# Graph attention and propagation in fp32: one ring of row tiles, a new table layout, and a new order of all steps

## The chip, the cores and the metric

The kernel runs on one core of one Trainium2 chip. The metric is the device time of one launch in microseconds. A span in this text is the time from the first to the last instruction of one profiled execution. PE is TensorE (PEld its weight loads), DVE is VectorE, ACT is ScalarE, POOL is GpSimd, SP is SyncE, which here issues DMAs only.

## What is computed

The input x has 32 batches of 512 channels by 1024 nodes, all in fp32; `adj` is 512 x 512. For each batch:

```
h = relu(layernorm(x))                       # over the 1024 nodes
q = wq . h ; k = wk . h                      # one number per node
scores[m, n] = leaky_relu(q[n] + k[m])       # slope 0.01
att = softmax(scores over n)
x = x + relu(adj @ (h @ att^T) + bm)
h = relu(layernorm(x))
x = x + adj^T-propagation of h (weights adj * adj) + bias
```

The scores depend on a sum of one number per row and one per column. The kernel uses this: with the nodes sorted by q, the softmax of a row is a suffix sum with one exponential factor plus a prefix sum with another, and the place where one ends and the other begins is a rank. No 1024 x 1024 matrix is formed.

## The kernel before

One batch goes through a long row of steps, each a small function. Names with a number in brackets at their line are those of the profile.

- `load` brings four tiles of 128 channels x 1024 nodes; `stats`, `norm`, `slopes`, `relu` normalise them (layer 0).
- `scores` (L445) computes q and k on PE; ACT copies them to `qr` (L450) and writes q to a small table in DRAM, `qd`; `row` reads it back to all partitions. `columns` turns q and k into columns.
- `rank` (L487 to L496, DVE) counts for each node how many are smaller; `to_rows` makes of it the row of a table in DRAM. `lower` (L503, ACT) and `from_rows` do the same for the place at which each node will look up its sums. `factors` makes the exponential factors.
- `value` (L550) multiplies h by adj transposed, eight steps of four products; `spread` copies out of PSUM; `scatter` (L563, POOL, an indirect DMA) writes the rows, sorted by rank, to the batch's table `td`.
- `fetch` (L580, SP) reads the sorted rows back as three tiles `vs` of three blocks. `weights` (ACT), `later` (DVE) and `stationary` (L623, POOL) make triangular matrices of weights, `totals` (L612) the denominators.
- `scan` (L639, L636) is nine steps: block `i` of the prefix sums and block `8 - i` of the suffix sums are two half-wide products that run side by side. `sums` (L648 to L655) carries the last row into the next block's tile, copies the result to one of two buffers `t` and writes it to `td` by two DMAs.
- `gather` (L660, POOL, indirect) reads for each node the row with its suffix sum, prefix sum and own sorted row. `excess`, `divide`, `weigh`, `combine` (L689) put them together.
- `reload` brings x again; `turn` (L696) transposes the result on PE and DVE adds it to x (L698); `stats`, `norm`, `slopes`, `relu` (layer 1), then `propagate` (L703), eight steps of four products, `finish` (L711) and the store.

A table `td` has nine blocks of 63 pairs of ranks. A slot of a pair is three rows: suffix sum, prefix sum, sorted value. Before, all even ranks' slots stand in the table's first half and all odd ranks' in its second, so that `fetch` needs one DMA for each half. There are five tables, used in turn. `pads` fills the slots that no rank takes, at the start.

The order is not that of the loops. `plan` gives every step of every batch a time: the batch's number times T plus an entry of the table PLAN, with corrections for the first five and last five batches (FIRST, LAST). All steps are sorted by that time and issued in that order; each engine then runs its own part of it in order, and waits where data or buffers aren't ready. SP issues all loads, reloads, fetches, `sums` writes and stores in one order. The DMAs of SP and ACT take turns on eight semaphores, so a DMA is issued only when the one eight before it has landed. Row tiles come from three pools: 7 for x, 7 for the reloaded x, 4 for the second h.

Of the kernel before, what the change touches and what calls it, by code (L numbers as in the profile page):

```python
# [9 lines left out]
F32 = mybir.dt.float32  # L10
# [3 lines left out]
ALU = mybir.AluOpType  # L14
AX = mybir.AxisListType

P = 128
# [4 lines left out]
PAIRS = 63  # L22
QUAD = 32
ROUND = 12582912.0
FAR = -1.0e30
TABLES = 5
PLAN = {
    "adjacency": (-108.2,),
    "biases": (103.637,),
    "columns": (-0.644,),  # L30
    "combine": (
        295.175, 296.981, 297.681, 298.56, 293.456, 294.898, 296.312, 299.441, 298.758,
        299.991, 297.356, 298.478, 299.289, 299.451, 296.18, 297.782,
    ),
    "compare_mask": (-39.924,),
    "divide": (279.776,),
    "excess": (274.084,),
    "factors": (31.052,),
    "fetch": (71.51,),
    "finish": (356.071, 361.635, 372.571, 377.123, 391.802, 417.732, 398.837, 420.531),  # L40
    "from_rows": (87.236,),
    "gather": (260.35, 264.453, 263.071, 264.447, 267.501, 263.458, 263.983, 262.344),
    "later": (82.669,),
    "lift": (343.707, 352.288, 361.264, 350.629),
    "load0": (-132.547,),
    "load1": (-83.561,),
    "load2": (-110.642,),
    "load3": (-58.45,),
    "lower": (25.135, 20.956, 15.44, 19.087, 14.733, 13.756, 46.166, 37.237),
    "masks": (-18.987,),  # L50
    "norm0": (-31.509,),
    "norm1": (326.35,),
    "pads": (-73.925,),
    "propagate": (346.423, 349.207, 352.169, 365.765, 371.233, 382.761, 381.981, 389.706),
    "rank": (17.984, 18.872, 20.129, 19.992, 25.594, 25.16, 26.367, 26.318),
    "reload0": (283.236,),
    "reload1": (289.947,),
    "reload2": (275.592,),
    "reload3": (294.126,),
    "relu0": (-21.389, -21.25, -20.652, -20.617),  # L60
    "relu1": (336.308, 336.463, 336.836, 338.53),
    "row": (1.149,),
    "scan": (88.672, 94.082, 102.974, 119.344, 135.342, 151.67, 171.394, 183.726, 197.836),
    "scatter": (49.236, 49.927, 49.759, 49.383, 53.226, 50.436, 50.301, 52.611),
    "scores": (-2.312,),
    "slopes0": (-23.106,),
    "slopes1": (327.104,),
    "spread": (10.418, 15.798, 4.081, 13.981, 26.765, 25.953, 18.654, 18.733),
    "square": (58.25,),
    "stationary": (82.87, 113.617, 158.362),  # L70
    "stats0": (-66.042, -57.278, -62.987, -37.25),
    "stats1": (317.836, 318.803, 321.449, 320.562),
    "sums": (90.354, 96.928, 115.433, 127.043, 139.894, 157.148, 175.982, 190.223, 211.407),
    "to_rows": (21.507, 28.041),
    "totals": (87.7,),
    "turn0": (305.575, 305.673, 305.631, 305.894),
    "turn1": (311.888, 311.406, 311.889, 311.693),
    "turn_adjacency": (-56.308,),
    "value": (4.654, 14.383, -2.141, 4.319, 19.868, 19.769, 15.801, 17.456),
    "weigh": (288.834, 288.645, 287.955, 288.582, 291.515, 291.657, 292.795, 290.433),  # L80
    "weights": (79.137,),
}
FIRST = {
    "columns": ((-42.337, 0), (-5.231, 0), (-2.394, 0), (1.4, 0), (-0.267, 0)),
    "combine": (
        (1.654, -0.5293), (1.005, -0.3379), (12.151, -0.5389), (4.662, 1.8664), (-2.717, -0.8902),
    ),
    "divide": ((-6.522, 0), (2.121, 0), (-5.673, 0), (4.125, 0), (-1.132, 0)),
    "excess": ((-1.018, 0), (2.997, 0), (-2.579, 0), (2.459, 0), (2.332, 0)),
    "factors": ((12.008, 0), (36.085, 0), (20.556, 0), (-17.001, 0), (38.59, 0)),  # L90
    "fetch": ((-13.827, 0), (-9.161, 0), (-4.562, 0), (-10.853, 0), (-1.955, 0)),
    "finish": (
        (-7.71, -0.5057), (2.749, -0.1853), (2.024, 0.1345), (-9.528, -0.7581), (-1.467, 0.1212),
    ),
    "from_rows": ((-16.545, 0), (143.901, 0), (-18.52, 0), (2.567, 0), (44.362, 0)),
    "gather": (
        (-9.577, -0.9485), (-11.32, -0.6577), (-4.449, 0.1722), (-9.629, -0.1251), (0.796, 0.0714),
    ),
    "later": ((-7.518, 0), (-7.347, 0), (-5.042, 0), (-3.972, 0), (4.883, 0)),
    "lift": (  # L100
        (18.493, -0.0414), (7.449, -0.8273), (15.021, 1.1896), (12.507, -0.3341), (13.391, 1.5716),
    ),
    "load0": ((-55.083, 0), (-28.454, 0), (-82.787, 0), (-89.755, 0), (-8.172, 0)),
    "load1": ((-101.05, 0), (-75.105, 0), (-63.613, 0), (-51.655, 0), (-0.85, 0)),
    "load2": ((-75.638, 0), (-49.315, 0), (-74.213, 0), (-72.717, 0), (-4.898, 0)),
    "load3": ((-124.613, 0), (-99.018, 0), (-53.784, 0), (-32.124, 0), (2.903, 0)),
    "lower": (
        (-42.973, -0.9302), (-15.708, -0.6946), (-9.312, -0.2971), (10.582, -0.0696), (34.856, -0.2988),
    ),
    "norm0": ((-83.601, 0), (-72.105, 0), (-7.68, 0), (-14.053, 0), (-0.379, 0)),  # L110
    "norm1": ((7.168, 0), (3.555, 0), (4, 0), (0.017, 0), (-5.5, 0)),
    "propagate": (
        (2.872, -0.6898), (4.018, -0.2375), (-1.06, -0.345), (-1.214, -0.2813), (-1.309, -0.0657),
    ),
    "rank": (
        (-28.589, 0.7379), (-2.87, -0.0721), (-9.055, 1.3394), (2.403, 0.1874), (-13.459, 0.0458),
    ),
    "reload0": ((-6.546, 0), (6.572, 0), (3.271, 0), (5.826, 0), (-6.189, 0)),
    "reload1": ((-1.43, 0), (8.813, 0), (6.594, 0), (3.913, 0), (-1.301, 0)),
    "reload2": ((-12.374, 0), (4.019, 0), (-0.514, 0), (8.006, 0), (-11.757, 0)),  # L120
    "reload3": ((1.756, 0), (10.208, 0), (8.663, 0), (2.721, 0), (1.743, 0)),
    "relu0": (
        (-45.821, -0.4234), (-30.012, 0.2683), (5.354, 1.299), (-1.745, 0.0153), (3.565, -0.5324),
    ),
    "relu1": (
        (9.188, 0.8499), (2.193, -0.013), (10.49, -0.8921), (-4.148, -0.0533), (5.006, -0.1977),
    ),
    "row": ((-24.758, 0), (-11.86, 0), (-11.402, 0), (-3.047, 0), (-12.236, 0)),
    "scan": (
        (-10.549, -0.0092), (-6.067, 0.0274), (-9.758, -0.1074), (-3.442, 0.0619), (-0.102, -0.002),  # L130
    ),
    "scatter": (
        (-17.315, 0.2618), (-11.153, 0.1679), (0.523, -0.1955), (-0.018, 0.156), (10.696, 0.3981),
    ),
    "scores": ((-62.327, 0), (-16.533, 0), (-8.214, 0), (-8.615, 0), (-9.042, 0)),
    "slopes0": ((-60.963, 0), (-35.582, 0), (0.527, 0), (-21.398, 0), (0.491, 0)),
    "slopes1": ((7.724, 0), (5.221, 0), (19.376, 0), (1.394, 0), (7.329, 0)),
    "spread": (
        (-20.028, 0.1376), (-6.015, 0.992), (8.718, 0.232), (10.947, -0.0528), (-1.297, 0.1468),
    ),  # L140
    "stationary": (
        (-9.533, -0.0517), (-0.489, 0.0893), (-5.756, -0.1735), (-6.449, -0.1248), (4.497, -0.0251),
    ),
    "stats0": (
        (-104.674, 0.702), (-77.356, 0.023), (-31.203, 0.8527), (-27.97, 0.4148), (-4.885, 0.5116),
    ),
    "stats1": (
        (1.142, 1.1308), (0.139, -0.1099), (5.326, 1.0258), (1.699, -0.7252), (-0.894, -0.2163),
    ),
    "sums": (  # L150
        (-8.312, -0.031), (-5.309, 0.0498), (-7.225, -0.0992), (-0.666, 0.0426), (1.428, -0.0107),
    ),
    "to_rows": (
        (-22.19, 0.5865), (-4.005, -0.1384), (-1.537, -0.1666), (6.658, -0.9288), (6.396, -0.6681),
    ),
    "totals": ((-8.637, 0), (-5.524, 0), (-8.905, 0), (-5.244, 0), (1.382, 0)),
    "turn0": ((-0.966, 0.9178), (2.05, 1.1944), (5.507, -0.2416), (13.541, 1.3559), (6.422, 0.711)),
    "turn1": (
        (-5.235, 2.5311), (3.046, 0.3048), (6.19, 0.6659), (-2.074, -0.6081), (-2.371, 1.8837),
    ),  # L160
    "value": (
        (-38.477, -0.2052), (-18.574, 0.6364), (-1.298, 0.5607), (-3.097, 0.6813), (-5.339, -0.0078),
    ),
    "weigh": (
        (-11.307, 0.6182), (-3.966, -0.0933), (3.637, 0.3643), (2.741, 0.6417), (-2.168, 0.2103),
    ),
    "weights": ((-7.839, 0), (-5.68, 0), (-3.274, 0), (-1.31, 0), (1.823, 0)),
}
LAST = {
    "columns": ((7.408, 0), (2.218, 0), (11.624, 0), (6.617, 0), (9.298, 0)),  # L170
    "combine": (
        (184.23, -0.647), (7.018, -0.6426), (4.54, 0.7582), (4.732, 1.7176), (6.572, -0.8403),
    ),
    "divide": ((175.719, 0), (2.439, 0), (-3.673, 0), (2.742, 0), (4.328, 0)),
    "excess": ((172.709, 0), (3.234, 0), (1.536, 0), (-5.245, 0), (8.713, 0)),
    "factors": ((-5.036, 0), (-12.606, 0), (17.188, 0), (-12.641, 0), (7.562, 0)),
    "fetch": ((5.667, 0), (1.995, 0), (5.156, 0), (-1.217, 0), (1.341, 0)),
    "finish": (
        (752.974, -0.831), (173.796, 0.1634), (35.432, 0.5906), (9.597, -0.1536), (9.066, 0.2434),
    ),  # L180
# [616 lines left out]
```

## Time and profile before

| | us |
|---|---|
| timed runs, median of three | 2374.95 (2371.89 to 2375.03) |
| span of the profiled execution | 2372.9 |
| the profiled execution's own time | not listed apart; the timed runs lie from 1.0 below to 2.1 above its span |
| PE busy | 2295.2 (97%) |
| DVE busy | 1952.6 (82%) |
| ACT busy | 1599.8 (67%) |
| DMA moved | 643.45 MB, mean 271 GB/s |

The slices of the page divide the span into forty parts; a digit is the busy share in tenths. The chain follows the last instruction back to what released it, step by step. The view by windows gives the busy time of each engine in chosen stretches.

### The profile page before, as it was taken

The numbers are of one execution on the slowest core, as the hardware profiler recorded it, in microseconds if no ns is written. First come the engines' busy times: TensorE is split into PE (matmuls) and PEld (weight loads), VectorE is DVE, ScalarE is ACT, GpSimd is POOL, SyncE is SP. The second block draws the span as 40 slices with busy tenths as digits, with TensorE's granted clock in tenths as the row PEclk, the third lists the DMA queues.
The fourth block names the chain that finished last, engine by engine and source line by source line (L and its number), as shares of the span: only waits on it lengthen the run. The fifth ranks groups of instructions, "written<-read, shape, count | busy, mean of one in ns | idle before, by whom it ended". The sixth has DMA issues, their size and how long they took to land.

```text
span 2372.9 us, 28069 instructions
## 1 busy us (share of the span) xinstructions
PE 2295.2 (97%) x7568; PEld 1011.5 (43%) x7568; DVE 1952.6 (82%) x5008; ACT 1599.8 (67%) x2880; POOL 720.7 (30%) x973
## 2 busy tenths in 40 slices
PE   7787999999999999999999999999999999999997
PEld 3233444444444444444444444444444444443443
DVE  7457888888888888888888888888888888888875
ACT  4576776766777766777676777676677676677551
POOL 2233333233333233233223233323333323233310
PEclk9988999999999999999999999999999999999998
DMA  6678888989999998999999999899988898998972
GB/s 222 171 181 277 284 284 277 296 269 276 287 290 285 296 286 266 277 299 283 288 292 266 276 294 287 287 291 272 268 291 276 288 302 253 276 282 269 311 294 79
DMA packets 206894, 643.45 MB, mean 271 GB/s; under 512 B 29120, under 2 KB 29248, under 8 KB 206736
## 3 DMA queue, kind: packets, MB, share of 16 engines
q1 hardware_dynamic: 142944, 355.74, 53.9%
q0 software_dynamic: 57344, 268.99, 30.7%
q10 hardware_dynamic: 6448, 16.92, 2.3%
q8 instruction: 61, 1.00, 0.2%
q14 instruction: 97, 0.79, 0.1%
HBM read 429.94 MB, written 211.60 MB: 270 GB/s over the span
## 4 chain that ended last, share of the span: by engine, by line
PE 85%; DMA 5%; DVE 5%; ACT 2%; issue 1%; POOL 1%; SPq 0%; ACTq 0%; another core or an unknown queue 0%; POOLq 0%; DVEq 0%
PE pg L703 34%; PE pv L550 33%; PE sc L639 10%; PE tr L696 4%; DMA vs<-td 2%; PE pq L445 2%; PE sc L636 1%; DVE g L689 1%; DVE st L414 1%; DMA g<-td,idg 1%; DMA td<-v,idx 1%; DVE junk L492 1%; ACT x L433 0%; DVE junk L487 0%; DMA x<-in_x_dram 0%
## 5 line engine op out<-in xcount | busy, mean ns | idle before, releaser
L703 PE MATMUL pg<-h,wsq 128*128 128x512 f32 x2048 | 911.2, 598 | 12.8 <-ACT h L433 12.8
L550 PE MATMUL pv<-wmT,x 128*128 128x512 f32 x2048 | 908.8, 598 | 5.9 <-ACT x L433 4.4
L703 PEld LDWEIGHTS pg<-h,wsq 128*128 128x128 f32 x2048 | 382.8, 191 | 517.4 <-issue 476.1
L550 PEld LDWEIGHTS pv<-wmT,x 128*128 128x128 f32 x2048 | 382.0, 191 | 499.1 <-issue 452.6
L623 POOL TENSOR_TENSOR sm<-mask_a,wc 128x192 f32<-128x192 f32 x96 | 51.9, 540 | 1254.9 <-DVE wc L600 785.7
L689 DVE SCALAR_TENSOR_TENSOR g<-g,cf 128x512 f32<-128x512 f32 x512 | 357.9, 756 | 46.4 <-ACT g L685 44.3
L648 ACT COPY vs<-sc 1x512 f32<-1x512 f32 x256 | 145.3, 567 | 272.9 <-PE sc L639 208.6
L563 POOL DMA_INDIRECT td<-v,idx x256 | 272.4, 1064 | 149.3 <-POOL v L562 36.3
L639 PE MATMUL sc<-vs,sm 128*64 128x512 f32 x1024 | 282.6, 621 | 21.3 <-POOL sm L623 11.1
L503 ACT ACTIVATE junk<-qrow,qk 128x1024 bf16<-128x1024 f32 x256 | 294.0, 1148 | 5.5 <-DMA qrow<-qd 2.5
L660 POOL DMA_INDIRECT g<-td,idg x256 | 243.5, 951 | 147.4 <-issue 71.5
L698 DVE SCALAR_TENSOR_TENSOR y<-tr,nbm,y 128x512 f32<-128x512 f32 x256 | 174.4, 744 | 66.3 <-PE tr L696 61.2
L711 DVE SCALAR_TENSOR_TENSOR y<-pg,bm_sb,y 128x512 f32<-128x512 f32 x256 | 185.8, 731 | 32.4 <-PE pg L703 32.0
L651 ACT COPY t<-sc 128x512 f32<-128x512 f32 x288 | 168.0, 583 | 40.7 <-DMA td<-t 35.3
L433 ACT ACTIVATE x<-x,nmr,rstd 128x1024 f32<-128x1024 f32 x128 | 148.6, 1231 | 64.9 <-DVE nmr L425 64.9
L492 DVE TENSOR_SCALAR_CACHE_REDUCE junk<-qrow,qk,cnt 128x896 bf16<-128x896 f32 (+6 forms) x224 | 180.5, 806 | 8.2
L685 ACT ACTIVATE g<-g,cf 128x512 f32<-128x512 f32 x256 | 167.7, 712 | 6.4 <-DVE cf L679 5.3
L487 DVE TENSOR_SCALAR_CACHE_REDUCE junk<-qrow,qk 128x128 bf16<-128x128 f32 (+6 forms) x224 | 166.0, 741 | 6.6
L414 DVE BATCH_NORM_STATS2 st<-x 128x6 f32<-128x512 f32 x256 | 162.7, 677 | 9.6 <-DMA x<-in_x_dram 9.6
L439 DVE TENSOR_TENSOR y<-y,bias_sb 128x1024 f32<-128x1024 f32 x128 | 154.3, 1219 | 16.0 <-ACT h L433 16.0
L557 ACT COPY v<-pv 128x512 f32<-128x512 f32 x256 | 141.8, 579 | 29.7 <-PE pv L550 14.0
L414 DVE BATCH_NORM_STATS2 st<-y 128x6 f32<-128x512 f32 x256 | 160.4, 668 | 0.0
(111 smaller groups left out, 1923.1 us busy)
## 6 DMA issues: line engine op xcount, KB each, us to landing
vs<-td SPq DMA_DIRECT2D x192, 384.8 KB
td<-t SPq DMA_DIRECT2D x576, 128.2 KB
x<-in_x_dram SPq DMA_DIRECT2D x128, 512.0 KB
y<-in_x_dram SPq DMA_DIRECT2D x128, 512.0 KB
out_dram<-y SPq DMA_DIRECT2D x128, 512.0 KB
qrow<-qd ACTq DMA_DIRECT2D x32, 512.0 KB
td<-v,idx POOLq DMA_INDIRECT x256, 8.3
g<-td,idg POOLq DMA_INDIRECT x256, 13.8
```

The costliest lines, as they stand in the source:

```text
L414: nc.vector.bn_stats(st[:, i, :], s.x[c][:, ts(i, HALF)])
L492: nc.vector.tensor_scalar(junk[:, j * P :], s.qrow[:, j * P :], qc, first, ALU.is_lt, ALU.add, accum_out=s.cnt[:, 1, j : j + 1],)
L503: nc.scalar.activation(junk, s.qrow, AF.Sign, bias=s.qk[:, 1, j : j + 1], accum_out=s.sgn[:, j : j + 1])
L550: nc.tensor.matmul(pv, s.h[c][:, ts(j, P)], wmT[:, c, :], start=(c == 0), stop=(c == NC - 1))
L563: i = nc.gpsimd.indirect_dma_start(tds[s.b % TABLES][:, :], bass.IndirectOffsetOnAxis(ap=s.idx[j // 4][:, j % 4 : j % 4 + 1], axis=0), v[: ...
L639: nc.tensor.matmul(p[ts(k, HP), :], m[:, k, :], s.vs[h][:, 0:C], start=True, stop=True)
L651: nc.scalar.copy(t[:, 0:C], p)
L660: nc.gpsimd.indirect_dma_start(s.g[:, j, :], None, tds[s.b % TABLES][0 : 3 * NB * HP, :].rearrange("(s k) w -> s (k w)", k=3), bass.Indire ...
L689: nc.vector.scalar_tensor_tensor(r, s.g[:, j, k * W : k * W + C], s.cf[:, k, j : j + 1], r, ALU.mult, ALU.add)
L698: nc.vector.scalar_tensor_tensor(xh, pt, nbm[:, o : o + 1], xh, ALU.max, ALU.add)
L703: nc.tensor.matmul(pg, wsq[:, r, ts(c, P)], s.h[r][:, ts(i, HALF)], start=(r == 0), stop=(r == NC - 1),)
L711: nc.vector.scalar_tensor_tensor(xh, s.pg.pop((c, i)), bm_sb[:, c : c + 1], xh, ALU.add, ALU.add)
```

## The change

Five things are changed together.

1. The three pools of row tiles become one of 18, for x, the reloaded x and the second h.
2. The table layout: even and odd ranks alternate by block, 64 slots each. `fetch` is now one DMA for all 128 partitions and three blocks: three DMAs for each batch instead of six. `to_rows`, `from_rows`, `sums` and `gather` follow the new layout; `from_rows` has one more operation.
3. Six tables instead of five and four `qd` rows instead of two.
4. `gather`'s source is now the whole table. A new step, `holes`, once for each table, copies part of x in DRAM to the rows of the odd slots that the sums never fill (9 blocks x 64 slots x 1026 numbers, 2.36 MB). `pads` becomes a step for each table, with its own pad tile.
5. Every time in PLAN, FIRST and LAST is new; FIRST and LAST now cover six batches.

```diff
-TABLES = 5
+TABLES = 6
+ROWS = 18
+QROWS = 4
 PLAN = {
-    "adjacency": (-108.2,),
+    "adjacency": (-1097.781,),
...
+    "holes": (34.897, 99.535, 87.359, 138.266, 176.285, 188.843),
...
-    "pads": (-73.925,),
+    "pads": (-39.033, -44.874, -89.13, -76.712, -133.381, -98.538),
...
-    xp = ctx.enter_context(tc.tile_pool(name="xp", bufs=7))
-    yp = ctx.enter_context(tc.tile_pool(name="yp", bufs=7))
-    hp = ctx.enter_context(tc.tile_pool(name="hp", bufs=NC))
+    xp = ctx.enter_context(tc.tile_pool(name="xp", bufs=ROWS))
...
     def sorted_rows(td, h, n):
-        rows = td.rearrange("(o h s k) w -> o s h k w", o=2, s=HP, k=3)
-        return rows[:, :, h : h + n, 2, :]
+        rows = td.rearrange("(h p k) w -> p h k w", p=P, k=3)
+        return rows[:, h : h + n, 2, :]
...
-    def pads(s):
-        pad = vp.tile([P, W], F32, tag="v", name="pad")
+    def pads(s, i):
+        pad = vp.tile([P, W], F32, tag="v", name=f"pad_{i}")
         nc.vector.memset(pad, 0.0)
         nc.vector.memset(pad[:, C : C + 1], FAR)
-        for td in tds:
-            for o in range(2):
-                nc.sync.dma_start(sorted_rows(td, 0, NB - 1)[o, 0], pad[0 : NB - 1, :])
-                nc.sync.dma_start(sorted_rows(td, NB - 1, 1)[o, :, 0], pad[0:HP, :])
+        for o in range(2):
+            nc.sync.dma_start(sorted_rows(tds[i], 0, NB - 1)[o * HP], pad[0 : NB - 1, :])
+        nc.sync.dma_start(sorted_rows(tds[i], NB - 1, 1)[:, 0], pad)
+
+    def holes(s, i):
+        rows = tds[i].rearrange("(h o s k) w -> h o s (k w)", o=2, s=HP, k=3)[:, 1, :, 0 : 2 * W]
+        flat = x.rearrange("b c n -> (b c n)")[0 : NB * HP * 2 * W]
+        nc.sync.dma_start(rows, flat.rearrange("(h s w) -> h s w", h=NB, s=HP))
...
-        odd = 3.0 * NB * HP
+        odd = 3.0 * HP
...
-        nc.vector.scalar_tensor_tensor(s.idx[i], block, 3.0, rk, ALU.mult, ALU.add)
+        nc.vector.scalar_tensor_tensor(
+            s.idx[i], block, 3.0 * (P - PAIRS), rk, ALU.mult, ALU.add
+        )
...
-        nc.vector.scalar_tensor_tensor(s.idg, pair, 1.0, block, ALU.add, ALU.add)
+        nc.vector.tensor_scalar(block, block, float(P - PAIRS), 1.0, ALU.mult, ALU.add)
+        nc.vector.tensor_tensor(s.idg, pair, block, ALU.add)
...
-            for o in range(2):
-                d = nc.sync.dma_start(t[ts(o, HP)], sorted_rows(tds[s.b % TABLES], 3 * i, 3)[o])
-                for k in s.sc:
-                    tc.add_manual_dep(d.ins, k.name, DONE, reason="any of them may hold a row")
+            d = nc.sync.dma_start(t, sorted_rows(tds[s.b % TABLES], 3 * i, 3))
+            for k in s.sc:
+                tc.add_manual_dep(d.ins, k.name, DONE, reason="any of them may hold a row")
...
-        nc.sync.dma_start(td[ts(ha, HP), 0, :], t[0:HP, :])
-        nc.sync.dma_start(td[ts(hb, HP), 1, :], t[HP:P, :])
+        nc.sync.dma_start(td[ts(2 * ha, HP), 0, :], t[0:HP, :])
+        nc.sync.dma_start(td[ts(2 * hb, HP), 1, :], t[HP:P, :])
...
-            tds[s.b % TABLES][0 : 3 * NB * HP, :].rearrange("(s k) w -> s (k w)", k=3),
+            tds[s.b % TABLES].rearrange("(s k) w -> s (k w)", k=3),
```

What the new order means for the steps that the prediction names (v: value, s: scan, t: turn, p: propagate, q: scores, c: columns, d: totals; the number is the batch). One period of PE in the steady part:

```
before  q15 v15 c15 v15x2 d14 s14 s13 s14 v15x5 s14 s13 p11x3 s13 s14 p11x2 s14 p11x2 t12x4 p11 t12x4 s14
after   q15 t11x8 v15 c15 v15x2 d14 s13 s14 v15x2 s14 v15x2 s13 s14 v15 p11x3 s14 s13 p11x2 s14 p11x3 s14
```

POOL in the head, and the end of PE's order:

```
before  scatter2x8 stationary1 stationary2 gather0x8 stationary2 scatter3x8 ...
after   scatter2x8 stationary1 gather0x7 stationary2 gather0 stationary2 scatter3x6 ...

before  ... p29x2 t30x8 p29x3 p30x8 t31x8 p31x8
after   ... p29 t30x8 p29x4 p30x8 t31x8 p31x8
```

In the head, PE's order between the first totals of batch 3 and the first propagate step is `s3 s2 v4x5 s3 s2 s3` before and `s2 v4x2 s3 v4 s3 s2` after. SP's order in the head is, after: the adjacency, batch 0's loads, loads and `pads` mixed, hole 0, fetch 0, hole 2, the first `sums` of batch 0, hole 1, two `sums`, two loads, a `sums`, hole 3, a `sums`, fetch 1, a `sums`, hole 4, three more `sums` and a reload, hole 5.

## The prediction

> **What bounds the kernel now.** I read the page first: busy rows, slices, chain.
>
> ```profile
> span 2372.9 us, 28069 instructions
> ...
> PE 2295.2 (97%) x7568; PEld 1011.5 (43%) x7568; DVE 1952.6 (82%) x5008; ACT 1599.8 (67%) x2880; POOL 720.7 (30%) x973
> ...
> PE   7787999999999999999999999999999999999997
> ...
> PEclk9988999999999999999999999999999999999998
> ...
> PE 85%; DMA 5%; DVE 5%; ACT 2%; issue 1%; POOL 1%; SPq 0%; ACTq 0%; another core or an unknown queue 0%; POOLq 0%; DVEq 0%
> ```
>
> PE is the bound, except in the first four or five slices and the last two. I cut the span at the first propagate product (263.4) and at the first PE idle of the end (2109.4). Columns: length, busy time of PE, PEld, DVE, ACT, POOL, granted clock, DMA share, GB/s.
>
> ```profile
> 0.00:263.40 263.40, 210.70 (x689) 87.13 (x689) 165.62 (x524) 163.61 (x307) 73.60 (x116) 0.94 0.75 224
> 263.40:2109.40 1846.00, 1845.25 (x6162) 817.85 (x6161) 1591.69 (x4083) 1310.16 (x2355) 594.65 (x789) 1.00 0.91 283
> 2109.40:2372.90 263.50, 239.22 (x722) 106.53 (x720) 195.26 (x403) 126.04 (x219) 52.44 (x69) 0.95 0.72 238
> ```
>
> PE idles 52.7 us in the head, 0.75 in the middle, 24.3 in the tail. The middle can gain only by PE's own order. The chain there shows the period (start, length):
>
> ```profile
> 1160.16 17.36 PE pv L550 x40
> ...
> 1230.69 17.36 PE pv L550 x40
> 1248.06 1.87 PE sc L639 x8
> ...
> 1284.01 1.01 PE sc L639 x4
> ...
> 1286.88 3.63 PE pv L550 x8
> ...
> 1297.94 3.28 PE sc L639 x12
> ```
>
> 1230.69 - 1160.16 = 70.53 us a batch. Thirty-two are 2257, so about 116 us of the span is head and tail: the room there is. In head and tail the chain leaves PE:
>
> ```profile
> 107.26 9.96 DMA vs<-td
> ...
> 180.13 16.16 DMA g<-td,idg
> ...
> 2127.12 8.65 DMA vs<-td
> ...
> 2140.85 0.38 ACT qr L450
> ...
> 2146.28 7.27 DMA qrow<-qd
> ```
>
> **What the Trainium skill says.** "DMA: Bandwidth & Descriptors", section "Why a DMA increments its semaphore by 16 and not by 1": a copy from SP runs on the largest number of engines up to 16 that divides the slowest dimension. The new `holes` copy is 9 x 64 x 1026, hence 9 engines; no transfer of that shape is in the trace. Same page, "Queues, rings and completion order": a queue's transfers are consumed in ring order on each engine, so the small `sums` writes sit behind a hole. The trace has only their usual landing (6.35 us). "TensorE: Matmul & The Clock Gate", "What's actually happening": idle PE drops to half clock. The trace agrees: 0.94 and 0.95 in head and tail, 1.00 between.
>
> **The change, part by part.**
>
> *Ring, pools, queue rows.* 7 + 7 + 4 tiles become one ring of 18, so the same memory. Following the new order, in the steady part a tile is taken at least 15 us of plan time after its last user; four `qd` rows and six tables only lengthen reuse. No wait of before names them. I take 0; cover is the next loads, already a batch ahead, and if it fails SP blocks and `sums` and `fetch` behind it are late.
>
> *Steady period.* Entering 64- or 32-wide products costs 0.15 us (one scan 1.01, two 1.87, so a scan is 0.86), leaving them 0.19 (eight products take 3.63 after scores, 3.44 after transposes): 0.34 a visit. Before makes four visits a batch, after five: +0.34. Before's three scans behind `totals` take 3.28 instead of 3 x 0.86 = 2.58: the third waits for the row that ACT carries over. After puts four value products between those two: -0.70. All eight `turn` steps now stand together: 3.5 us of PE fills eight banks, which DVE empties at 0.68 each, so the first value product behind them takes a bank freed about when it comes: 0 to 0.3, I take 0.2; if DVE is late with `combine` up to 0.9. One more DVE operation in `from_rows` (0.17) hides in DVE's 9 us of idle. Sum -0.16 a period, over some 25: **-4** (-9 to +14).
>
> *Head.* (1) The adjacency (1.05 MB at 283 GB/s, 3.7 us) is loaded ahead of batch 0, but its transposes (2.25) leave the way: values start about 2 later, batch 0's scores 3.7 later. (2) `pads` are six memsets of 0.49, the last three inside batch 0's ranks, and both `to_rows` come after all ranks. Scatter of batch 0, 36.8 to 50.5 before, I put at 51 to 65; it also needs hole 0, whose place in SP's order (12 MB behind it or in it, at 283) lands about 45 to 50. This is a new wait: behind that scatter on POOL stand batch 0's `stationary` steps, and for them wait its scans. `square` (3.61 on POOL) moves ahead of the scatter, to where POOL is idle until 36.8: 0. Batch 0's fetch lands near 80 instead of 68. (3) A fetch is three issues instead of six of 0.65: SP free, and the last landing, 2 us sooner, four times in the head. (4) Six holes of 2.36 MB. On nine engines each carries 262.7 KB; in the steady part an engine moves 283/16/0.91 = 19.4 GB/s: 13.5 us a hole, 81 for all, mostly between 70 and 165. Before, the DMAs were 61% to 78% busy from 50 to 160, so some 30 to 35 us of this fits, the rest delays what stands behind it: `fetch` 1, and `sums`, whose two `t` buffers make ACT, and then the next scan, wait. Bounds: 0 to +40 on the last scan of batch 0; I take +15. (5) Against this: gather 0 started at 171.4 behind `stationary` of batch 2, though its last row had landed at about 152.5; now seven of eight gathers stand ahead of that step. That is up to -19. From (2), (4) and (5) the last gather lands about when it did (before 196.8): -7 to +20. (6) The rest hangs on that landing, since batch 3's `to_rows` stands behind `excess` of batch 0 on DVE in both orders: scatter 3, fetch 3, first totals of batch 3 at 237 before, 235 now. (7) Between those totals and the first propagate product before had five value steps and five scans (26.5 us); after has three and four: 15 us, the other values being done while fetch 3 lands. Batch 0's `slopes` no longer stands behind five ranks (its relu ran at 253.7, 12 us behind its statistics), so it's ready. First propagate: 235 + 15 = 250 against 263.4: **-13** (-22 to +25).
>
> *Tail.* From the last scores on, both orders have the same products; the chain scores 31, rank, scatter, fetch, scan, gather, combine, propagate is as long as before. ACT copied `qr` 31 at 2140.85, 5.7 us after its products ended at 2135.1, because `weights` 30 stood ahead and waited for the fetch; now `scores` and `row` stand ahead. Of the 5.7 perhaps 3 arrives, since batch 31's second `to_rows` still waits behind `excess` 28 and its gather. One more propagate step of batch 29 covers the 3.4 us idle before batch 30's, but the last gather sets the end anyway. **-3** (-9 to +6).
>
> Sum: -4 - 13 - 3 = -20; 2372.9 - 20 = 2353. The timed runs have a median of 2374.95, 2 above the profiled span: **2355**.
>
> **Rivals.** *A: the holes block SP's ring.* Should they push batch 0's last gather from 197 to 225 or later, the head turns from -13 to +15; with the waits of later batches behind them and the other terms, 2370 to 2395, about 2386. It decides from a landing near 217, where 20 us of gain are gone. For it: nine engines, an in-order ring, two `t` buffers. Against it: half the DMA time is free then, and the gather had 19 us to spare. *B: the gain is hidden.* The first propagate comes sooner, but values 5 or turn 1 then wait for gather 1 and the gain is spent by 320, or DVE's late `combine` costs 0.5 a period: about 2374. *C: the holes are cheap* (landing at 185) and the tail passes on its 5.7: head -24, tail -8, steady -8: 2335. *D: what it says isn't done* is excluded for the fetches (three per batch in the new order).
>
> **How the numbers follow.** Main case 0.52 (its own range 2341 to 2367), A 0.26, B 0.11, C 0.11. About 0.2% (4.7 us) is what a measurement here can tell from no change: B is mostly within. Faster 0.63, same 0.11, slower 0.26. The range takes in C's centre and most of A: 2333 to 2389.
>
> **What would show it.** Right: period 70.2 to 70.6; `sc` behind `pd` without a wait for ACT; first propagate near 250; PE idle in the head about 40 us; `vs<-td` 96 issues; holes landing in 13 to 25 us; ACT's wait for `td<-t` longer than before's 35.3 us. Wrong: first propagate past 270, or a period over 71, or PE waits in the middle third of over 5 us.

## The result, and the profile after

The changed kernel takes **2436.57 us** (median of 4 runs, 2433.26 to 2441.38) against 2374.99 us for the kernel before beside it: a ratio of **1.026** (95% interval 1.0243 to 1.0276), slower. The forecast was 2355 us with a range of 2333 to 2389, so the time lies outside the range, on the other side of no change.

The page of the changed kernel, with the lines that answer to those shown of before:

```profile
span 2439.5 us, 27967 instructions
...
PE 2294.1 (94%) x7568; PEld 1006.3 (41%) x7568; DVE 1954.7 (80%) x5050; ACT 1587.5 (65%) x2874; POOL 711.9 (29%) x973
...
PE   7756998999999999999999999999999999999797
...
PEclk9878999999999999999999999999999999999899
...
PE 77%; DMA 13%; DVE 5%; ACT 2%; issue 1%; POOL 1%; SPq 0%; ACTq 0%; DVEq 0%; POOLq 0%
```

PE's busy time is what it was (2294.1 against 2295.2), and every instruction count of PE is the same. The span grew by 66.6 us, so all of it is idle PE. The slices show where: among the first seven and the last three. In the chain, DMA rose from 5% to 13%.

The same cuts as in the prediction, the last one up to this kernel's end (columns: stretch, length, busy time of PE, PEld, DVE, ACT, POOL, granted clock, DMA share, GB/s):

```profile
0.00:263.40 263.40, 177.54 (x578) 73.81 (x582) 140.18 (x449) 141.21 (x263) 62.98 (x103) 0.86 0.75 239
263.40:2109.40 1846.00, 1825.47 (x6077) 802.06 (x6070) 1576.02 (x4079) 1286.80 (x2329) 572.05 (x780) 0.99 0.83 280
2109.40:2439.50 330.10, 291.09 (x919) 130.39 (x917) 238.51 (x524) 159.53 (x284) 76.87 (x90) 0.95 0.66 235
```

PE now idles 85.9 us in the first stretch (52.7 before), 20.5 in the middle one (0.75 before) and 39.0 in the last (24.3 before).

The chain of waits in the steady part, where PE's products run without a gap (start, length). The `scores` products of two batches following each other stand 1256.55 - 1186.37 = 70.18 us apart, against 70.53 before:

```profile
1186.37 1.86 PE pq L632 x32
...
1256.55 1.86 PE pq L632 x32
```

The chain in the head, its DMA waits (start, length; such a line ends with the landing):

```profile
91.16 18.40 DMA td<-t
...
119.88 12.93 DMA td<-v,idx
...
134.01 9.81 DMA vs<-td
...
147.76 11.08 DMA td<-t
...
162.40 25.02 DMA td<-t
...
196.57 21.98 DMA vs<-td
```

Before, this chain went through one landing of `td<-t` up to here, of 6.35 us. Now there are three, of 11 to 25 us, and the fetch of batch 2 (the last line) takes 22 us to land where that of batch 1 takes 9.81 here and took 9.96 before.

PE's longest waits (what it waited for: us in all, times, longest):

```profile
PE pd L801 <- ACT w L778: 41.9, 5, 14.0
PE sc L825 <- ACT vs L838: 25.9, 2, 21.5
PE sc L828 <- ACT vs L837: 25.4, 3, 16.3
```

The engine named is ACT, but `w` and `vs` are ACT's steps behind a fetch and behind a free `t` buffer: both wait for a DMA.

To place the loss I cut the two spans at the first `propagate` product of batches 0, 8, 22 and 26. The two middle columns are kernels from the experiments below (both with three tables instead of six, one in the order of before, one in the new order). All in us, of the profiled executions:

| stretch | before | new layout, old order, 3 tables | new order, 3 tables | changed kernel |
|---|---|---|---|---|
| to propagate 0 | 263.3 | 259.1 | 267.6 | 292.3 |
| 0 to 8 | 563.4 | 563.0 | 576.5 | 581.8 |
| 8 to 22 | 987.4 | 987.3 | 982.7 | 983.9 |
| 22 to 26 | 282.9 | 282.8 | 290.0 | 290.9 |
| 26 to the end | 275.9 | 270.5 | 289.8 | 290.6 |
| span | 2372.9 | 2362.7 | 2406.6 | 2439.5 |

From column to column one part of the change is added. Layout (with the ring, the `qd` rows, three tables and their copies): -10.2, the timed runs say -6.5. Order: +43.9, timed +41.5. Three more tables with their `holes`: +32.9, timed +28.3.

A reading of one profiled execution of a crowded head is good to some 6 us: two of the kernels below (with the last batches' times of before, and with `weights` moved in batch 31) have the changed kernel's head step for step, and their propagate 0 starts at 289.0 and 286.0 instead of 292.3.

### The profile page after: what moved, and what is told of

Same layout as the page of the kernel before. It is cut to its first block, busy times and chain, and to the rows that moved or that the text cites. A ratio compares the mean times of both kernels' runs of the same rounds, so it can differ in the third digit from the quotient of the medians.

```text
span 2439.5 us, 27967 instructions
## 1 busy us (share of the span) xinstructions
PE 2294.1 (94%) x7568; PEld 1006.3 (41%) x7568; DVE 1954.7 (80%) x5050; ACT 1587.5 (65%) x2874; POOL 711.9 (29%) x973
## 4 chain that ended last, share of the span: by engine, by line
PE 77%; DMA 13%; DVE 5%; ACT 2%; issue 1%; POOL 1%; SPq 0%; ACTq 0%; DVEq 0%; POOLq 0%
PE pg L892 31%; PE pv L740 29%; PE sc L828 9%; DMA vs<-td 5%; PE tr L885 4%; DMA td<-t 3%; PE pq L632 2%; DMA x<-in_x_dram 2%; DMA g<-td,idg 1%; DVE g L878 1%; PE sc L825 1%; DMA out_dram<-y 1%; DVE st L602 1%; DMA td<-v,idx 1%; ACT x L620 1%
## 5 line engine op out<-in xcount | busy, mean ns | idle before, releaser
L740 PE MATMUL pv<-wmT,x 128*128 128x512 f32 x2048 | 922.4, 602 | 0.7 <-ACT x L620 0.7
L753 POOL DMA_INDIRECT td<-v,idx x256 | 279.4, 1091 | 410.4 <-DVE rk L710 167.5
L878 DVE SCALAR_TENSOR_TENSOR g<-g,cf 128x512 f32<-128x512 f32 x512 | 363.2, 784 | 6.3 <-ACT g L874 6.3
L812 POOL TENSOR_TENSOR sm<-mask_a,wc 128x192 f32<-128x192 f32 x96 | 57.0, 594 | 1031.2 <-DVE wc L789 633.9
L828 PE MATMUL sc<-vs,sm 128*64 128x512 f32 x1024 | 274.1, 628 | 29.2 <-ACT vs L837 25.4
L840 ACT COPY t<-sc 128x512 f32<-128x512 f32 x288 | 168.1, 584 | 91.8 <-DMA td<-t 83.7
L679 DVE TENSOR_SCALAR_CACHE_REDUCE junk<-qrow,qk,cnt 128x512 bf16<-128x512 f32 (+6 forms) x224 | 180.5, 806 | 8.2
L674 DVE TENSOR_SCALAR_CACHE_REDUCE junk<-qrow,qk 128x512 bf16<-128x512 f32 (+6 forms) x224 | 164.1, 733 | 24.7 <-DMA qrow<-qd 18.5
L874 ACT ACTIVATE g<-g,cf 128x512 f32<-128x512 f32 x256 | 160.9, 712 | 11.9 <-DVE cf L868 11.8
L620 ACT ACTIVATE h<-y,nmr,rstd 128x1024 f32<-128x1024 f32 x128 | 153.2, 1244 | 12.0 <-DMA out_dram<-y 6.6
```

Source lines behind the costliest of these rows:

```text
L620: nc.scalar.activation(h, s.x[c], AF.Relu, bias=s.nmr[:, c : c + 1], scale=s.rstd[:, c : c + 1])
L679: nc.vector.tensor_scalar(junk[:, j * P :], s.qrow[:, j * P :], qc, first, ALU.is_lt, ALU.add, accum_out=s.cnt[:, 1, j : j + 1],)
L740: nc.tensor.matmul(pv, s.h[c][:, ts(j, P)], wmT[:, c, :], start=(c == 0), stop=(c == NC - 1))
L753: i = nc.gpsimd.indirect_dma_start(tds[s.b % TABLES][:, :], bass.IndirectOffsetOnAxis(ap=s.idx[j // 4][:, j % 4 : j % 4 + 1], axis=0), v[: ...
L828: nc.tensor.matmul(p[ts(k, HP), :], m[:, k, :], s.vs[h][:, 0:C], start=True, stop=True)
L878: nc.vector.scalar_tensor_tensor(r, s.g[:, j, k * W : k * W + C], s.cf[:, k, j : j + 1], r, ALU.mult, ALU.add)
```

## The experiments

Theory H was that the `holes` copies hold up SP's queue; theory O that the new order of steps loses by itself; others are named as they come. Times are medians; ratios, with their 95% intervals, are to runs of the kernel before beside them.

**1. Which part of the change is it?** Four kernels: the changed one with its copies on sixteen engines; the layout of before in the new order, no copies; the new layout in the order of before; the kernel before with six copies of that size added (its tables merged to one row of 576 slots).

```
- rows = ...rearrange("(h o s k) w -> h o s (k w)", ...)[:, 1, :, 0 : 2 * W]   # 9 x 64 x 1026
+ rows = ...rearrange("(h o s k) w -> o s h (k w)", ...)[1, :, :, 0 : 2 * W]   # 64 x 9 x 1026
```

> The changed kernel (2436.6 us) with one edit: the holes copy is written with the slot as its slowest dimension (64 x 9 x 1026 instead of 9 x 64 x 1026), so that, by the Trainium skill's rule on how many engines a copy uses, it runs on 16 engines instead of 9; same bytes, same place. Theory H (the holes block SP's ring because nine engines carry 262.7 KB each): the writes of sums behind a hole land in under 12 us instead of 18 to 25, the first propagate step comes 15 to 40 us sooner, 2398 to 2420 us. Theory O (the new order is slower by itself, holes or not): 2430 to 2440 us. Rival B (the bytes matter, not the engines): 2425 to 2436.

2421.31 us (1.0216, 1.0195 to 1.0238): 15 less than the changed kernel, propagate 0 at 277.9 instead of 292.3. The trace agrees with the number of engines: as it lands, a copy raises its semaphore sixteen times here, and nine times (and once just after its issue) in the changed kernel. But writes behind a copy still take up to 21 us to land. The engines matter, and they aren't all of it.

```
  before.py with PLAN, FIRST, LAST of the changed kernel, ROWS = 18, TABLES = 6, QROWS = 4, no holes, six fetch transfers
```

> The changed kernel's order of steps, ring, six tables and four qd rows with the table layout of before: six fetch transfers a batch, no holes. Theory H: the head loses its extra 50 us, the tail's 25 us stay: 2380 to 2396 us, first propagate step near 250. Theory O: 2420 to 2436 us, first propagate step past 280.

2472.34 us (1.0415, 1.0397 to 1.0432): without a single copy, the slowest of all. Propagate 0 starts at 266.8, but 0 to 8 takes 602 us, and the tail has two waits of 22 and 24 us. The order (with the ring, the tables and the `qd` rows, which cost nothing in the old order below) loses 100 us on the old layout: worse than O's own figures.

```
  changed kernel with PLAN, FIRST, LAST of before; holes at 20, 76, 76, 126, 165, 176; pads at -73.925
```

> The changed kernel with the step times (PLAN, FIRST, LAST) of before; holes are put at the same places among the fetches and sums as in the changed order. Theory H: the holes delay the head of the old order as well: 2405 to 2425 us, tail as before. Theory O: 2370 to 2390 us, and the old order with one ring, six tables and three fetch transfers is as fast as before or a little faster.

```
  before.py with TABLES = 6 and six copies of 2.36 MB at the same times
```

> The kernel before (2375.0 us) with six tables and with the six holes copies added and nothing else; in its layout the rows to fill are one stretch of 576 slots, so the copy runs on 16 engines. It is the price of 14.2 MB in the head by itself. Theory H with nine engines as the cause: 2378 to 2390 us (16 engines pass them sooner). Rival B (bytes): 2400 to 2425 us. Theory O: within 5 us of before.

2402.18 us both (1.0127, 1.011 to 1.0144, and 1.0124, 1.0107 to 1.0141). So in the order of before six copies cost 30 us, on nine engines or sixteen, as rival B had it, and the layout itself nothing that shows. Both H and O hold in part.

**2. Where does each part lose?** The first two of these keep the changed kernel but take some batches' times from the tables of before; the other two move hole i to just ahead of batch i.

```
+ old = s.b < OLD_HEAD or s.b >= OLD_TAIL
+ plan_, first, last = (OLD_PLAN, OLD_FIRST, OLD_LAST) if old else (PLAN, FIRST, LAST)
+ shift += OLD_SHIFT if old else 0            # 13.0
- "holes": (34.897, 99.535, 87.359, 138.266, 176.285, 188.843),
+ "holes": (34.9, 85.6, 166.3, 246.9, 327.6, 408.2),          # in the old order 20.0, 72.6, 153.3, 233.9, 314.6, 395.2
```

> The changed kernel, but the last six batches (26 to 31) take every step's time from the kernel before's tables, shifted by 13 us of plan time, which is the distance of the two plans. Theory P (the loss is a sum of parts that stand by themselves: holes in the head about 28 us, the new order of batches 1 to 5 about 18, the new order of the last batches about 28, less some 5 in the steady part): the tail's part goes, 2436 - 28 = 2408 (2400 to 2416), and the last propagate products end within 515 us of the start of batch 24's, as before's do. Rival R (the tail is late because the one ring of 18 tiles makes ACT and SP wait for stores, whatever the order): 2428 or more, with ACT waiting for an out_dram<-y landing again.

2427.35 us (1.0221, 1.0198 to 1.0244). From propagate 26 to the end it takes 269.4 us, 21 less than the changed kernel, where theory P said 28, but the joint costs: 22 to 26 takes 304 us instead of 291, so the whole misses P's figures. The ring of 18 tiles isn't the cause; rival R falls.

> The changed kernel, but the setup steps and the first six batches (0 to 5) take every step's time from the kernel before's tables, shifted by 13 us of plan time; the six holes stay early, at 20 to 176 us of that plan. Theory P: batch 0's propagate still starts near 292 to 297, since the holes are still there, but batch 8's starts near 860 instead of 874: 2436 - 14 = 2422 (2415 to 2428). Rival Q (the later stalls of batches 1 to 5 are the holes' own and come in either order): batch 8 near 874, 2432 to 2440.

2432.33 us (1.0248, 1.0223 to 1.0274): propagate 0 at 295.6, propagate 8 at 867.8. That is 6 us of the 14 that P wanted, no more than two executions of one head differ. Inconclusive.

> The changed kernel with its own order; only hole i is moved from the first 190 us of plan time to 5 us after the start of batch i's period, about 50 us ahead of batch i's scatter, so that the same six copies on nine engines lie between the loads of batches 1 to 5. Theory P: batch 0's propagate starts at 262 to 270 instead of 292, the order's own losses stay: 2408 (2400 to 2418). Rival Q (the stalls of batches 1 to 5 are the holes' too): 2386 to 2398. Rival O (the new order loses by itself, the holes only fill its gaps): 2425 to 2436.

> The new layout (one ring, three fetch transfers, six tables, holes) in the kernel before's order, as in the earlier run at 2402, with hole i moved to 8 us ahead of batch i's period. Theory P: all that the holes cost is queueing in the head, and the layout by itself gives or takes nothing: 2372 to 2380, batch 0's propagate near 263 to 268. Rival B (bytes cost wherever they are: 2.36 MB at 283 GB/s is 8.3 us a hole): 2385 to 2402.

2428.5 us (1.0221, 1.0197 to 1.0245) and 2404.8 us (1.0124, 1.0102 to 1.0146). Spread over five batches the copies cost as much as at the front in the order of before (2404.8 against 2402.18). In the new order the kernel gains 8 us: propagate 0 starts at 279.1 instead of 292.3, but 0 to 8 and the tail get no shorter. In the order of before the chain shows how the copies still cost: a load issued behind the hole at 175 us landed 29.07 us later, batch 3's ranks waited behind its statistics on DVE (207.9 instead of 178.3 in the kernel before), and batch 0's `excess` behind them (222.9 instead of 196.8). Theory P is too simple: propagate 0 came at 296.1, not at 263 to 268.

**3. Queue, count, and one wait of the tail.**

```
- nc.sync.dma_start(rows, flat...)
+ nc.scalar.dma_start(rows, flat...)
```

> The changed kernel with the six holes issued from ACT's queue instead of SP's, at the same places of the order; bytes, shape and the nine engines as they are. Theory Q (what costs is standing behind a hole in SP's ring): sums writes, fetches and loads no longer wait for a hole, batch 0's propagate starts at 268 to 276 instead of 292, 2412 to 2422. Theory B (the 14.2 MB take DMA time wherever they are queued): propagate still at 285 or later, 2430 to 2440.

> The new layout in the kernel before's order (2402 with the holes on SP's queue), holes on ACT's queue. Theory Q: 2376 to 2388, batch 0's propagate at 265 to 278 instead of 297. Theory B: 2398 to 2406.

2452.98 us (1.0335, 1.0313 to 1.0356) in the new order and 2406.95 us (1.0145, 1.0124 to 1.0166) in the old: a loss of 16 in the one, no gain in the other. But two things keep these runs from deciding on theory Q. ACT reaches hole 0 later than SP (48.0 us against 30.3 in the old order), so batch 0's scatter starts 13.5 us later. And the copies still hold up SP, since its DMAs and ACT's take turns on the same eight semaphores. In the old order SP waits 30.3 us for copies that stand in ACT's queue, against 7.9 when they stand in its own (us in all, times, longest; L658 and L659 are the two writes of `sums`):

```profile
SPq L659 <- DMA td<-in_x_dram: 17.5, 1, 17.5
SPq L658 <- DMA td<-in_x_dram: 12.8, 2, 7.8
```

The landings tell more. The Trainium skill's "DMA: Bandwidth & Descriptors" has it under "Queues, rings and completion order", as I took it in the prediction, that a queue's transfers are consumed in ring order on each engine, and the traces agree. In the changed kernel the three long landings of `td<-t` in the head's chain come at 109.6, 158.8 and 187.4 us, each less than 1 us after the landing of a copy that was issued ahead of it (108.8, 158.2 and 186.9 by the copies' semaphores). A write issued at 188.2, with no copy left, landed in 2.3 us. With the copies on ACT's queue (old order), writes issued at 157.0 and 157.9 landed at 165.2 and 168.1, ahead of the copy issued at 155.5, which landed at 175.0. So standing in SP's ring holds these writes up; how much of the price it makes stays open, since no run frees SP of the copies altogether.

```
- TABLES = 6
+ TABLES = 3            # three pads, and "holes": (20.0, 76.0, 76.0)
```

> The new layout in the kernel before's order with three tables instead of six, and so three holes (at 20, 76 and 76 us of plan time) and 7.1 MB instead of 14.2. If each hole costs the same, half of the 30 us goes: 2387 (2383 to 2391). If the first three, which lie where batches 0 and 1 wait for their transfers, do all of it: 2398 to 2404. If it is the last three, in front of batch 0's sums and gather: 2374 to 2380. A scatter that had to wait for the gather three batches ahead would show in the steady part as a period over 70.6.

**2366.77 us (0.9974, 0.9966 to 0.9983): faster than the kernel before**, and 35 us less than with six tables. That is more than half of the copies' price: the first three cost next to nothing, the last three all of it. The steady part kept its period (987.3 over 14 batches), so three tables are enough.

```
- "weights": ((13.914, -1.472), ...     # LAST, batch 31
+ "weights": ((21.914, -1.472), ...
```

> The changed kernel with one time changed: batch 31's weights 8 us later in the plan, so that on ACT they stand behind batch 28's four relu1 instead of ahead of them. Theory W (in the tail ACT stands still at weights 31 until fetch 31 lands, 20 us after its issue, and relu1 28 and with it the only propagate products left wait behind it: 16.3 us of PE idle): 10 to 16 us less, 2420 to 2426. Rival G (the end hangs on fetch 31, its scans and its gather, which come no sooner): 2432 to 2440, the idle time only moves.

2430.9 us (1.025, 1.0225 to 1.0276): 5.7 us less, with intervals that overlap. The wait of 16.3 us became one of 10.9 for the same fetch, and from propagate 26 to the end the profile has 286.5 us instead of 290.6. The head, which the edit doesn't touch, changed by more (286.0 instead of 292.3), so a gain isn't shown. The 10 to 16 us of theory W didn't come; the figures of G are the nearer ones.

**4. Place or number, and the new order without late copies.**

> The changed kernel in its own order with three tables instead of six: the three holes it keeps lie at 34.9, 99.5 and 87.4 us of plan time, those at 138, 176 and 189 are gone. Theory L (a hole costs where the DMA engines are full and batch 0's sums, the next fetch and the next loads are waited for, from about 110 us on; earlier it is nearly free): batch 0's propagate starts at 258 to 268 instead of 292, and what the new order loses by itself in batches 1 to 5 and in the tail stays, about 18 + 20 less 6 in the steady part: 2400 to 2412. Rival S (each hole costs about the same): 2416 to 2424. Rival O (the order loses all of it): 2428 to 2436.

2408.27 us (1.0137, 1.0113 to 1.0161), propagate 0 at 267.6: inside theory L's figures, but see the next run for its reason.

```
- "holes": (20.0, 76.0, 76.0),
+ "holes": (20.0, 76.0, 165.0),
```

> The kernel of 2366.8 us (new layout, order of the kernel before, three tables) with its third hole moved from 76 to 165 us of plan time, which is about 110 us into the run or later instead of 65; same bytes, same count. Theory L (place): batch 0's propagate 8 to 20 us later, 2375 to 2387. Rival S (bytes or count): no change, 2364 to 2370.

2365.7 us (0.9969, 0.9955 to 0.9982), propagate 0 at 256.3. A copy issued at 122.1 us costs no more than one at 65.3. L falls: it is not the place.

> The kernel of 2366.8 us with its three holes' slowest dimension 64 instead of 9, so that each copy runs on sixteen engines. PE idles 15 us at 91 us in that kernel, waiting for ACT's vs, where the kernel before idles 3 and 2. If that is the nine engines: 2 to 8 us less, 2359 to 2365. If the early holes are free, or it is their bytes: 2365 to 2369.

2365.95 us (0.996, 0.9948 to 0.9973): where three copies fit, nine engines or sixteen make no difference.

**5. Copies or tables?** Six copies as in the run at 2402, but `tds[s.b % 3]` everywhere, so that the last three copies go to tables which no batch uses:

> The new layout in the kernel before's order, with all six holes of the run at 2402 at their places, but the batches take turns on the first three tables only, as in the run at 2367: the last three copies go to tables that no batch uses. Theory N (the DMA time of the copies: about three fit beside the rest of the head, and each further one delays batch 0's last sums and its gather): as slow as with six tables, 2395 to 2404, batch 0's propagate at 288 to 298. Rival T (not the copies but what six tables bring: a first scatter into each that waits for its own hole and pads): 2364 to 2372.

2399.6 us (1.0115, 1.0094 to 1.0137), propagate 0 at 294.0. The copies are the cause, not that batches use six tables. (The three further `pads` are in this kernel too; all of theirs are issued before 27 us.) The chain of this kernel in the head, and under it that of the same layout and order with three copies (start, length):

```profile
126.45 16.65 DMA vs<-td
...
151.38 16.88 DMA td<-t
...
169.53 20.36 DMA td<-t
```

```profile
78.23 25.48 DMA td<-t
...
149.47 6.76 DMA td<-t
...
182.43 16.18 DMA g<-td,idg
```

With three copies the writes of `sums` that are issued from 74 to 85 land late, at 104, just after the third copy, and the rest of the head makes that up: the next lands in 6.76 us, and the gather ends the chain as in the kernel before. With six, writes and a fetch keep taking 17 to 20 us to land up to 190, and nothing is left to make it up. There is no fixed price per copy here: the head has room for three. A fourth can be enough: in the spread run of the old order, four copies before 200 us and one at 250 brought propagate 0 to 296.1.

> The changed kernel with three tables and three holes (2408 in its own order), its batches 0 to 5 and 26 to 31 on the kernel before's times shifted by 13 us, batches 6 to 25 on the new ones. If the loss that is left in the new order lies in its first and last batches: 2367 less 6 for the steady part, plus up to 17 for the two joints between the plans (7 and 10 us were seen with one joint each): 2362 to 2382. If the joints or the ring of tiles lose it whatever the ends: 2395 to 2410.

2395.2 us (1.0093, 1.0074 to 1.0111), beyond the expected range. Its ends are as good as those of before (propagate 0 at 261.3, from 26 to the end 272.6), but the joints cost 12 us before batch 8 and 21 us from 22 to 26. The two orders couldn't be joined by this shift.

**6. The gather of the new order's head.** Three tables, and batch 0's gathers 1 us earlier in the plan, so that the eighth no longer stands behind batch 2's `stationary` on POOL.

```
- "gather": ((-24.127, 0.058), ...      # FIRST, batch 0
+ "gather": ((-25.127, 0.058), ...
```

> The changed order with three tables (2408.3) and one more edit: batch 0's gathers 1 us earlier in the plan, so that on POOL the eighth, too, stands ahead of batch 2's first stationary step; in the run at 2408 it was issued at 196.3 us, 19 us behind the seventh, because that step waited for batch 2's weights. Theory G (the eighth gather sets batch 0's excess, and with it on DVE batch 3's to_rows, its scatter, fetch and totals, and the first propagate): excess of batch 0 at 188 to 195 instead of 206.8, the first propagate at 252 to 260 instead of 267.6, 2393 to 2402. Rival F (batch 3's totals come no sooner, since its ranks, values and transfers are as late without it): propagate at 264 to 268, 2404 to 2411.

2407.18 us (1.0129, 1.0104 to 1.0154). The eighth gather was issued at 176.0 instead of 196.3, and nothing followed: `excess` of batch 0 at 206.3 (206.8), propagate 0 at 267.2 (267.6). Theory G falls, F's figures hold. A kernel of the changed order without any copies on the new layout was not tried.

The trace shows what batch 3 hangs on instead: on DVE, `later` of batch 2 stands ahead of six of batch 3's eight ranks, and waits for fetch 2: DVE stands idle for 10.2 us there, while the eight gathers are under way. The queues while fetch 2 is under way in the changed kernel (196 to 219 us; packets, MB, share of 16 engines):

```profile
q0 software_dynamic: 973, 5.30, 57.0%
q1 hardware_dynamic: 1651, 3.39, 38.6%
q10 hardware_dynamic: 152, 0.53, 5.6%
```

And in the new layout with three tables in the old order (162.5 to 171 us):

```profile
q1 hardware_dynamic: 1377, 2.68, 91.6%
```

q0 carries POOL's gathers, q10 ACT's transfers, and q1 SP's, fetch 2 among them. In the new order batch 0's seven gathers are issued with fetch 2, and take 57% of the engines' time while it waits: 22 us to land. In the old order they are issued after it has landed, in some 8 us. With three tables on both sides the gathers come only 5 us earlier in the new order (168.9 against 173.6), and the fetch 8 us later (170.4 against 162.5); both bring them together. The engines' time is as good as full in both windows. That this collision is the cause is read from the traces; no run takes the gathers away from the fetch.

## Why the prediction was wrong, and where it was right

The span's 66.6 us lie in these places: 29.0 up to propagate 0 (-13 forecast), 18.4 from there to propagate 8 (nothing forecast), -3.5 over the next 14 batches, 8.0 from propagate 22 to 26 (nothing forecast) and 14.7 from there to the end (-3 forecast).

*Steady period: right in kind.* -0.16 a batch was forecast; 70.53 became 70.18, and 14 batches took 983.9 instead of 987.4. With three tables on both sides it is 982.7 against 987.3. That is -0.25 to -0.35 a batch, some twice the sum.

*Ring, pools, queue rows, fetch in three: small, and better than forecast.* With three tables the layout gives 6.5 us in the timed runs: propagate 0 comes 4.2 earlier, the end 5.4.

*Head, (1), (2) and (7): sizes held.* Batch 0's scatter ran from 55.2 to 66.6 (51 to 65 forecast), its totals at 80.3 (80). Scores came 6 later instead of 3.7. Between batch 3's totals and propagate 0 lay 292.3 - 277.5 = 14.8 us (15 forecast, 24.7 before).

*Head, (4): the kind right, the size off.* +15 with a bound of 40 was taken; six copies put propagate 0 24.7 us later than three in the new order, and 37.8 in the old one (296.9 against 259.1). So with six copies the old order's head is no faster than the new one's: this term is most of what the changed kernel's head lost. Single copies took 18 to 26 us to land, near the 13 to 25 expected. The working took the copies' time from the average free share of DMA, as if each byte had the same price; but the DMA share of the first stretch is 0.75 in both kernels, so the engines weren't full on average. The spare copies show a limit instead: about three fit, and the others go straight to the critical writes and fetches, which stand behind them in SP's ring.

*Head, (5) and (6): the steps that failed.* The prediction gave gather 0's earlier place up to -19 and hung batch 3's totals on its landing: 235. (Its own terms, +12 from (2), +15 and -19, add up to +8 for that landing, where it took none.) The totals came at 277.5, and at 252.8 with three copies. The gather isn't what they hang on: moving its last row by 20 us moved nothing. By the chain they hang on fetch 2, whose totals came at 218.9 (194.8 with three copies, 169.4 before), and the gathers are what fetch 2 now shares the engines with. I had counted what the moved step waits for, and not what its transfer collides with.

*Batches 1 to 7, and 22 to 25: not in the prediction at all.* 18.4 us are lost between propagate 0 and 8, and PE idles 13.5 us between 263 and 700, mostly for fetches (of batches 4 and 5) that land in 14 and 20 us. What the 8.0 us from 22 to 26 hang on was not taken apart. "The middle can gain only by PE's own order" was true; that it can lose in another way was left out.

*Tail: the step that failed* is "the chain is as long as before". From propagate 26 to the end the new order takes 19.3 us more than the old one on the same layout. Counted from propagate 26, batch 31's scores end at 38 as before, but its scatter ends at 100.2 instead of 85.7 (new layout, old order, three tables) and its last fetched row is used at 128.8 instead of 109.1. The 5.7 us that `qr` 31 waited are gone, as the prediction had it. But ACT copies batch 31's last value 12.9 us after the products, against 1.6, and then the fetch takes 20 us:

```profile
2252.44 3.64 PE pg L892 x8
...
2256.88 20.31 DMA vs<-td
...
2277.70 2.26 ACT h L620 x2
```

While it lands PE runs out of propagate products, since `relu1` of batch 28 stands behind `weights` 31 on ACT. Undoing that one wait gave no gain that is shown; what is left is the late fetch. While it is under way (2256 to 2278 us) gathers take most of the engines' time, as in the head; in the old order it lands in 6.3 us (three tables, by its semaphore):

```profile
q0 software_dynamic: 989, 5.37, 59.9%
```

Which of ACT's steps makes its issue late was not taken apart.

*Rivals.* A came nearest in kind: gather 0 landed past 217, and its mechanism, standing in SP's ring, is what the landings of the `sums` writes show. But it priced little beyond the head (about 2386), and how much of the copies' price is the ring's stays open. The loss of the order itself, 41.5 us, was in no rival. The order of before on the new layout with three tables is the best version run, 0.3% to 0.4% faster than the kernel before in three variants (2366.77, 2365.7 and 2365.95).

## What to carry to other kernels

When transfers are moved, ask what is in flight at that moment and who waits for it, and not only what the moved transfer was waiting for. Set-up copies need not have a price per byte: here three were free, while the slack of the head lasted, and three more cost 28 to 35 us, so first make fewer of them. Ask also what stands behind a large copy in its queue, and which waits two queues share. And an order written out by hand belongs to its layout: the same order lost 100 us on the old layout and 41 on the new one, and pieces of the two orders lost at their joints most of what each gained.

## What the hardware showed that I had not expected

- In SP's queue, small writes issued behind a 2.36 MB copy landed less than 1 us after it, 11 to 25 us after their issue (2.3 us with no copy left); with the copies in ACT's queue writes overtook them.
- Moving 14.2 MB of copies from SP's queue to ACT's gave no gain all the same (2406.95 against 2402.18 in the old order): SP then waited 30.3 us for them through the shared semaphores.
- Sixteen engines instead of nine gave 15 us in the new order, where six copies were too many, and nothing (2365.95 against 2366.77) where three fit. The prediction had priced a copy by the engine rule of the Trainium skill ("DMA: Bandwidth & Descriptors", "Why a DMA increments its semaphore by 16 and not by 1"); measured, the number of copies decides first.
- A fetch of 2.3 MB landed in about 8 us alone and in 22 beside gathers on the software queue (20 at the end of the run), with the engines' time full in both cases (91.8% and 101% by the queues' shares).
